# Layer 1 of a two-layer graph transformer on one NeuronCore: hand-laid memories, expert weights under tensors that end early, the residual assembled inside the second products, and routing by blocks

## The chip, the cores and the metric

The kernel runs on one NeuronCore of a Trainium2 chip, in one launch. The metric is device time in microseconds (us). Besides the run times there is one profiled execution of the kernel, whose trace gives the start and length of every instruction. Engines are named as the profile names them: PE is the matrix engine (PEld its weight loads), DVE the vector engine, ACT the scalar engine, POOL the general engine, SP the engine that here only starts DMA transfers; "SPq" or "POOLq" is such an engine's instruction queue.

## The reference, cut to what matters

Two layers work on x, 1250 rows of 512 numbers. Only the end of layer 1 is touched:

```python
xn = layernorm(x)
# graph part: agg is a 1250 x 1250 edge-count product
h  = (1 + eps) * xn + agg(xn)
h  = relu(batch_norm(h @ W1 + b1))      # 512 -> 1024, statistics over the 1250 rows
h  = relu(batch_norm(h @ W2 + b2))      # 1024 -> 512
gnn = xn + h
# slice attention, 8 heads of 64, 32 slices
xm = xn @ W_in + b_in
q, k, v = softmax(xm @ Wq), softmax_over_rows(xm @ Wk), xm @ Wv
mix = (q @ (k.T @ v)) @ W_out + b_out
x  = x + gnn + mix
# experts: each of 32 takes the 39 rows that the router scores highest for it
xf = layernorm(x)
S  = softmax(xf @ W_router + b_router)          # 1250 x 32
G, idx = top_k(S.T, 39)
up = xf[idx] @ W_up[group] + b_up               # 8 groups of 4 experts share W_up, 512 x 1365
y  = silu(up) @ W_down[expert] + b_down         # 32 matrices, 1365 x 512
x  = x.at[idx].add(G * y)
```

The expert weights are 8 W_up matrices of 2730 KB and 32 W_down matrices of 2816 KB (with their bias row). [...]

## The kernel before

A scheduler orders the instructions of each engine, mostly by the order of the program and by when operands are ready; inside a `manual_schedule` block the named engines keep the program's order. Each engine then runs its own queue in order and waits on semaphores. A tile pool is a piece of on-chip memory; a pool that is put where a released pool lay waits until the released pool's last reader is done. Pools on the "right" side grow from the top of the memory, and the tiles of one pool lie in it upwards in the order in which they are made.

The 1250 rows are ten tiles of 125 rows (`NT`, `TP`). `BLOCKS` groups them in 4, 4 and 2, so a block is 500, 500 or 250 columns of a transposed tensor. Four blocks of 128 features (`ND`) make 512; the 1024 hidden features are eight. A matrix product in float32 shows up as two PE records per matmul.

Layer 1 in order of time:

- **Preparation (L1099 to L1119).** SP loads the 1250 x 1250 count matrix `AT`, which has a pool of its own at the top of the memory. For each tile DVE computes the layer norm `xn3`; ACT rounds it to `xh`; POOL computes the remainder `xl = xn3 - xh` (L1118); PE transposes `xn3` to `xT`. Five `xn3` buffers rotate.
- **Aggregation (L1129)**: for each block and each 128 features, ten matmuls with `xh` and then ten with `xl` go into one PSUM bank; DVE adds `(1+eps) * xT`.
- **x_mid (L1149)**, then the **first products**: eight feature blocks `zT[m]` of the hidden layer, with the attention's pieces (`keys`, `queries_values`, `keys_values`) put between them on PE.
- **Second products (L1289 to L1303)**: four feature blocks of `gT`. For each, ACT adds the bias, DVE takes batch statistics (`batch_norm`), ACT applies the relu, and DVE adds `b_out` and `xT` (L1301).
- **finish(b) (L1319)**: for each tile, PE brings the four feature blocks of `gT` back to rows by matmuls with the identity (L1327) and adds the attention product `qsT @ kvW` in the same PSUM bank (L1329); DVE adds `xr` (L1330). Row statistics and the norm `xf` follow. POOL writes the row tile to `out` and `xf` to the DRAM tensor `xd`.
- **route(b) (L1340)**: PE transposes `xf`, multiplies with the router's weights (L170, 32 columns wide), and each tile goes through a softmax by itself; the 32 x 1250 scores end in `pT`. The finish of block n+1 stands ahead of the route of block n, and the scheduler may interleave them.
- **Top-k (L1382)**: five rounds on DVE, then the index tables, then the gather of the first token rows from `xd` (L1415).
- **Experts (L1426)**: per group 44 up matmuls (88 records) and 88 down matmuls of 39 rows (176 records), the weighted rows being added to `out` by an indirect DMA (L1458).

Eight slots of 22 KB per partition hold expert weights; `load(slots)` issues as many loads as the slots passed to it allow, in the order up, four downs, up, ... The first two slots (`expa`) are in the memory of the attention's temporaries, four (`expb`) where the 512 x 512 weights and `xr` lay, two (`expc`) where row tiles of the finish lay. A slot is loaded again when the matmuls that read it are done.

## Time and profile before

| | us |
|---|---|
| median of 3 runs | 1592.73 |
| lowest, highest | 1590.1, 1593.69 |
| the profiled execution, its own time | 1594.62 |
| its span (first to last instruction) | 1592.8 |

Landmarks in the profiled execution, from its timeline:

| what | from | to |
|---|---|---|
| aggregation on PE | 956.8 | 1004 |
| first products and attention pieces | 1047 | 1137.1 |
| second products | 1137.1 | 1206.4 |
| finish and route, until the top-k can start | 1206.4 | 1266.8 |
| top-k, index tables, first tokens | 1266.8 | 1299.5 |
| experts, first to last matmul | 1299.5 | 1576.7 |

Rows by stretch give for each engine the busy time and the number of instructions in brackets, then the granted PE clock (1.00 is full speed), the busy share of the DMA engines and what they moved in GB/s. Timeline rows give start, length, engine, line, operation, output<-inputs and count; what stands in square brackets is the idle time before it and what ended it. Group rows give busy time and mean length of one in ns, then the idle time ahead.

### The profile page before, as it was taken

How to read it: one execution, taken by the hardware profiler on the slowest of the kernel's cores; microseconds unless marked ns; L12 is line 12 of the kernel's file. 1: busy time of each engine (PE TensorE's matmuls, PEld its weight loads, DVE VectorE, ACT ScalarE, POOL GpSimd, SP SyncE). 2: the span in 40 equal slices, each digit the busy share in tenths (PEclk: the TensorE clock that was granted, in tenths of full speed). 3: DMA queues.
4: the chain of work that ended last, by engine and by line, in shares of the span. 5: the costliest groups of instructions: out<-in, count | busy, mean ns of one | idle time of the engine just before them, and what ended most of it. 6: DMA issues, size and time to landing. Idle time of an engine off the chain costs nothing. (4 is left out here: it accounts for less than half of the span.)

```text
span 1592.8 us, 15977 instructions
## 1 busy us (share of the span) xinstructions
PE 1450.2 (91%) x6218; PEld 783.2 (49%) x6218; DVE 670.5 (42%) x1476; ACT 400.9 (25%) x821; POOL 396.3 (25%) x308
## 2 busy tenths in 40 slices
PE   6999999999996999999999879999999649998895
PEld 3645744556664543222224338556655545564452
DVE  6313072457883453767667361245325430110000
ACT  1201110222332112444445310056321211111110
POOL 6100332000001200877787420000003102222111
PEclk9999999999997999999999999999999669999998
DMA  7100000001112300000000220000302589999994
GB/s 204 33 29 15 23 27 0 7 25 27 44 32 60 106 27 27 1 1 1 1 0 1 111 80 1 1 27 27 143 0 85 188 305 354 373 383 381 378 389 164
DMA packets 83009, 162.60 MB, mean 102 GB/s; under 512 B 17857, under 2 KB 19009, under 8 KB 82919
## 3 DMA queue, kind: packets, MB, share of 16 engines
q1 hardware_dynamic: 75031, 146.75, 25.9%
q0 software_dynamic: 6592, 14.44, 3.4%
q8 instruction: 54, 0.88, 0.2%
q10 hardware_dynamic: 1296, 0.23, 0.1%
q14 instruction: 36, 0.29, 0.1%
HBM read 147.48 MB, written 13.93 MB: 101 GB/s over the span
## 5 line engine op out<-in xcount | busy, mean ns | idle before, releaser
L937 POOL TENSOR_TENSOR acc<-acc,pT 125x1000 f32<-125x1000 f32 (+1 forms) x96 | 187.3, 1951 | 31.4 <-ACT pT L927 26.6
L1449 PE MATMUL ps_dn<-expw,act 128*39 128x512 f32 x704 | 161.9, 609 | 14.8 <-DMA expw<-in_W_down 14.8
L927 ACT ACTIVATE pT<-sc,sh 125x500 f32<-125x500 f32 (+1 forms) x240 | 132.7, 604 | 128.1 <-PE sc L919 118.4
L764 DVE TENSOR_REDUCE nms<-ps_nat 125x1 f32<-125x512 f32 (+1 forms) x240 | 128.5, 584 | 77.7 <-PE ps_nat L762 76.6
L919 PE MATMUL sc<-qT,kT 64*125 64x500 f32 (+1 forms) x480 | 117.9, 559 | 0.4 <-ACT sh L792 0.4
L945 PE MATMUL ps_o<-pT,va 125*64 125x500 f32 (+1 forms) x480 | 111.9, 545 | 0.0
L1449 PEld LDWEIGHTS ps_dn<-expw,act 128*39 128x39 f32 x704 | 44.0, 119 | 126.3 <-issue 107.0
L1435 PEld LDWEIGHTS ps_up<-tT,expw 128*128 128x128 f32 (+1 forms) x704 | 95.5, 191 | 6.6 <-issue 5.8
L1435 PE MATMUL ps_up<-tT,expw 128*128 128x156 f32 (+1 forms) x704 | 97.7, 302 | 0.5 <-ACT tT L1422 0.5
L1456 DVE TENSOR_SCALAR wgt<-ps_dn,pgat 39x512 f32<-39x512 f32 x32 | 24.0, 749 | 171.1 <-PE ps_dn L1449 170.6
L1458 POOL DMA_INDIRECT out_x<-wgt,sidx x32 | 45.3, 1417 | 182.1 <-DMA out_x<-wgt,sidx 88.1
L1438 ACT ACTIVATE act<-ps_up,vec 128x156 f32<-128x156 f32 (+1 forms) x88 | 34.3, 390 | 219.5 <-PE ps_up L1435 219.5
L513 DVE TENSOR_SCALAR os<-iota,smod,sval 125x626 bf16<-125x626 int16 x160 | 70.5, 441 | 3.8 <-PE ps_a L528 2.4
L163 PE MATMUL ps_f<-hT,l1w 128*128 128x500 f32 (+1 forms) x192 | 68.7, 513 | 0.0
L163 PE MATMUL ps_f<-zT,l1w 128*128 128x500 f32 (+1 forms) x192 | 67.6, 513 | 0.0
L528 PE MATMUL ps_a<-os,od 125*128 125x314 bf16 x392 | 66.1, 298 | 0.0
L919 PEld LDWEIGHTS sc<-qT,kT 64*125 64x125 f32 x480 | 36.9, 183 | 55.3 <-ACT pT L927 43.9
L762 PE MATMUL ps_nat<-kTr,qTr 64*125 64x512 bf16 (+1 forms) x240 | 49.1, 347 | 12.2 <-DVE nms L764 9.7
L828 POOL DMA_INDIRECT a_wk<-in_wk,rows x4 | 4.1, 1018 | 216.9 <-issue 216.9
L945 PEld LDWEIGHTS ps_o<-pT,va 125*64 125x64 f32 x480 | 24.3, 136 | 64.2 <-issue 63.9
L937 POOL TENSOR_TENSOR acc<-pT 125x1000 f32<-125x1000 f32 (+1 forms) x12 | 23.4, 1952 | 124.6 <-ACT pT L927 124.5
L163 PEld LDWEIGHTS ps_f<-zT,l1w 128*128 128x128 f32 x192 | 36.2, 189 | 31.1 <-issue 29.8
(365 smaller groups left out, 2239.3 us busy)
## 6 DMA issues: line engine op xcount, KB each, us to landing
expw<-in_W_down SPq DMA_DIRECT2D x28, 2816.0 KB
expw<-in_W_up SPq DMA_DIRECT2D x8, 2730.0 KB
expw<-in_W_down SPq DMA_DIRECT2D x4, 1536.0 KB
AT<-atd SPq DMA_DIRECT2D x9, 625.0 KB
atd<-ATd SPq DMA_DIRECT2D x10, 546.9 KB
expw<-in_W_down SPq DMA_DIRECT2D x4, 1280.0 KB
l1w<-in_l_W SPq DMA_DIRECT2D x4, 1024.0 KB
out_x<-x2r POOLq DMA_DIRECT2D x10, 224.0 KB, 2.7
```

Of the source, the lines that this page charges most:

```text
L163: nc.tensor.matmul(ps[:, :width], w(k)[:, m * P:(m + 1) * P], xT(k), start=k == 0, stop=k == nk - 1)
L513: nc.vector.tensor_scalar(oss[c % len(oss)][:, :HN + 1], iota[:TP, :HN + 1], smod[:, c:c + 1], sval[:, c:c + 1], ALU.is_equal, ALU.mult)
L528: nc.tensor.matmul(pss[d][:, n, :HALF], ods[c][:, a:a + P], oss[c % len(oss)][:, n * HALF:(n + 1) * HALF], start=c == CHUNKS[d][0], stop=c ...
L762: nc.tensor.matmul(pss[e][:TP, :z - y], qTr[r, c, i * TP:(i + 1) * TP], kTr[r, c, y:z], start=True, stop=True)
L764: nc.vector.tensor_reduce(nms[n][:, j, e, a:a + 1], pss[e][:TP, :z - y], AX.X, ALU.max)
L919: nc.tensor.matmul(scs[n, k][e][:, :w], kT[r, c, k * TP:(k + 1) * TP], qT[r, c, span(b)], start=True, stop=True)
L927: nc.scalar.activation(pT[:, e, :w], sc[:, :w], AF.Exp, bias=shs[n])
L937: nc.gpsimd.tensor_tensor(a, pTs[n, 0][:, :, :w] if k == 1 else a, pTs[n, k][:, :, :w], ALU.add)
L945: nc.tensor.matmul(os_[n][e * DH:(e + 1) * DH, :w], vn[:, k, h * DH:(h + 1) * DH], pTs[n, k][:, e, :w], start=k == 0, stop=k == NT - 1,)
L1435: nc.tensor.matmul(ps[:fw, :4 * CAP], wu[:, k, f * P:f * P + fw], tT[:, k, :], start=k == 0, stop=k == ND - 1)
L1449: nc.tensor.matmul(ps[j * 64:j * 64 + CAP, :], act[:, f, (2 * a + j) * CAP:(2 * a + j + 1) * CAP], expw["down", pair][j][:, f, :], start=f ...
L1458: nc.gpsimd.indirect_dma_start(out=out[:, :], out_offset=bass.IndirectOffsetOnAxis(ap=sidx[:CAP, e:e + 1], axis=0), in_=wgt[r, :], in_offs ...
```

## The change

The tensors of layer 1 and the expert slots no longer have pools of their own. Three memories are laid out by hand: `bm` (which holds `xr` and the four 512 x 512 weight places), `lb` and `la`. `at(m, a, ...)` is a view into one of them. There are again eight slots, now lying under tensors that end at different times:

- slot 1 under `xT`, 2 under `xmT` and a part of `kn`, 3 under the attention's temporaries, 4 under `qsT` and `kvW`, 5 under most of `zT`, 6 under three weight places, 7 under `gT`, 8 under `xr`;
- `load(1)` stands behind x_mid, `load(3)` behind the first products, `load(4)` in the second products, `load(6)` behind them, `load(8)` behind the routing. Down matrices are loaded one by one rather than in pairs.

`AT` now shares the pool `xn3p` with `xh`, `xl` and the five `xn3` buffers. `xT` is no longer needed at the end: POOL adds `xn3` to `xr` in the preparation. In the second products PE also does the attention product of each tile (`attended`) and the transposes of each finished feature block (`rows`), and DVE adds both to `xr` and takes the statistics in pieces of 128 features. After the last feature block come the row statistics of all ten tiles together and then, block by block, `normed` and `route`; the softmax handles a block at once. This part now stands inside the `manual_schedule` of PE. The last hidden block `zT[7]` lies where the second half of `l1_W1` lay, so its three bias steps are held back until that block's products are done.

```diff
-    resp = tc.alloc_tile_pool(name="resp", bufs=1)
+    base = ctx.enter_context(tc.tile_pool(name="base", bufs=1))
...
+    bm = base.tile([P, NT * D + 4 * ND * D], F32, name="bm")
+    xr = bm[:TP, :NT * D].rearrange("p (i d) -> p i d", d=D)
...
+    SLOT = NF * D
+    lb = ctx.enter_context(tc.tile_pool(name="l1memb", bufs=1)).tile([P, 2 * SLOT], F32, name="lb")
+    REST = 4 * SLOT
+    BREST = SLOT
+    LOADS = [w for g in range(NG) for w in (("up", g), *(("down", 4 * g + j) for j in range(4)))]
...
-        atp = tc.alloc_tile_pool(name="atp2", bufs=1, side="right")
-        AT = atp.tile([P, NT, N], F32, name="AT1")
+        xp = tc.alloc_tile_pool(name="xn3p", bufs=1, side="right")
+        AT = xp.tile([P, NT, N], F32, name="AT1")
...
+        xh = xp.tile([TP, NT, D], F32R, name="xh3")
+        xl = xp.tile([TP, NT, D], F32R, name="xl3")
...
+                nc.gpsimd.tensor_tensor(xl[:, i, :], xn[i], xh[:, i, :].bitcast(F32), ALU.subtract)
+                nc.gpsimd.tensor_tensor(xr[:, i, :], xr[:, i, :], xn[i], ALU.add)
...
+        la = ctx.enter_context(tc.tile_pool(name="l1mema", bufs=1)).tile([P, REST + 3736], F32, name="la")
+        SLOTS = [at(m, a, SLOT) for m, a in (
+            (lb, 0), (la, 0), (la, SLOT), (la, 2 * SLOT), (la, 3 * SLOT), (bm, NT * D + 4 * ND * D - SLOT), (lb, SLOT), (bm, 0)
+        )]
...
+        load(1)
...
+                    while held and (m < 2 * ND - 1 or b == BLOCKS[-1]):
+                        b_, ps = held.pop(0)
+                        nc.scalar.activation(zT[m][:, span(b_)], ps, AF.Identity, bias=v_("b1", m))
...
+            load(3)
+            def attended(i):
+                s = slice(i * TP, (i + 1) * TP)
+                mm_N(
+                    psum, [(qsT[:, j, s], kvW[:, j, :]) for j in range(2)],
+                    lambda ps: nc.vector.tensor_add(xr[:, i, :], xr[:, i, :], ps),
+                )
+            def rows(m, b):
+                ps = psum.tile([TP, 4, P], F32, name="ps_x", tag="mm")
+                v = xr[:, b[0]:b[0] + b[1], m * P:(m + 1) * P]
+                for i in tiles_of(b):
+                    nc.tensor.transpose(ps[:, i - b[0], :], gT[:, m, i * TP:(i + 1) * TP], ident)
+                nc.vector.tensor_add(v, v, ps[:, :b[1], :])
+                for i in tiles_of(b):
+                    nc.vector.bn_stats(st[:, i, m, :], xr[:, i, m * P:(m + 1) * P])
+            todo = [(attended, i) for i in range(NT)]
...
+                    if m and b == BLOCKS[0]:
+                        todo += [(rows, m - 1, b_) for b_ in BLOCKS]
+                    for _ in range(2 if m == 0 else 3):
+                        if todo:
+                            f, *x = todo.pop(0)
+                            f(*x)
+                    if m == 1 and b == BLOCKS[-1]:
+                        load(4)
...
-                    nc.vector.scalar_tensor_tensor(
-                        gT[:, m, span(b)], gT[:, m, span(b)], v_("b_out", m), xT[:, m, span(b)], op0=ALU.add, op1=ALU.add
-                    )
+                    nc.vector.tensor_scalar(gT[:, m, span(b)], gT[:, m, span(b)], v_("b_out", m), None, ALU.add)
+            load(6)
...
+            for b in BLOCKS:
+                rows(ND - 1, b)
+            for i in range(NT):
+                nc.vector.bn_aggr(mv[:, i, :], st[:, i, :, :])
+            nc.scalar.activation(rs[:, :, 0], mv[:, :, 1], AF.Sqrt, bias=eps5[:TP])
...
+            def normed(b):
+                for i in tiles_of(b):
+                    xf = xfs[i] = at(bm, BREST + i % 4 * D, D, p=TP)
+                    if i % 2:
+                        nc.scalar.activation(xf, xr[:, i, :], AF.Identity, bias=rs[:, i, 1:2], scale=rs[:, i, 0:1])
+                    else:
+                        norm(xf, xr[:, i, :], mv, rs[:, :, 0], i)
+                for i in tiles_of(b):
+                    put_rows(xd, i, xfs[i])
+                    put_rows(out, i, xr[:, i, :])
...
+                for i in range(n):
+                    for k in range(ND):
+                        nc.tensor.matmul(
+                            ps[:, i, :], xfT[:, k, i * TP:(i + 1) * TP], wr[:, k, :], start=k == 0, stop=k == ND - 1
+                        )
...
+                nc.vector.tensor_tensor(pr, ps[:, :n, :], bias.to_broadcast([TP, n, NE]), ALU.add)
+                nc.vector.tensor_reduce(su[:, :, 0], pr, AX.X, ALU.max)
+                nc.vector.tensor_tensor(pr, pr, su.to_broadcast([TP, n, NE]), ALU.subtract)
+                nc.scalar.activation(pr, pr, AF.Exp)
+                nc.vector.tensor_reduce(su[:, :, 0], pr, AX.X, ALU.add)
                 nc.vector.reciprocal(su, su)
-                nc.vector.tensor_scalar(pr, pr, su, None, ALU.mult)
+                nc.vector.tensor_tensor(pr, pr, su.to_broadcast([TP, n, NE]), ALU.mult)
...
+            for b in BLOCKS:
+                normed(b)
+                route(b)
+    load(len(SLOTS))
...
-        load(sum(ROOM) + 5 * g + 1)
+        load(len(SLOTS) + 5 * g + 1)
...
-            load(sum(ROOM) + 5 * g + 2 * a + 3)
+            load(len(SLOTS) + 5 * g + 2 * a + 3)
```

In the expert stage `tok`, `act`, `tT` and `wgt` become views into `la` and `bm` with the same number of buffers as before.

## The prediction

> **What bounds the kernel now.** I read the page's slices first, then the engines by stretch, then the groups, the timeline around each stage boundary, and the granted clock in steps of 2 us.
>
> ```profile
> PEclk9999999999997999999999999999999669999998
> DMA  7100000001112300000000220000302589999994
> GB/s 204 33 29 15 23 27 0 7 25 27 44 32 60 106 27 27 1 1 1 1 0 1 111 80 1 1 27 27 143 0 85 188 305 354 373 383 381 378 389 164
> ```
>
> One slice is 39.8 us. DMA is nearly idle until slice 31 (it begins at 1195 us) and full from slice 34 (1314) on: the expert weights are the only heavy transfer, and they come late. The clock drops in slices 32 and 33, which hold the end of the routing and the top-k.
>
> ```profile
> 1137.00:1208.00 71.00, 71.00 (x219) 38.50 (x219) 18.85 (x51) 15.78 (x26) 0.37 (x3) 1.00 0.22 80
> 1208.00:1267.00 59.00, 48.97 (x237) 36.70 (x235) 31.46 (x94) 16.23 (x42) 21.82 (x41) 0.79 0.43 141
> 1267.00:1299.00 32.00, 1.93 (x10) 1.39 (x10) 22.10 (x33) 0.42 (x1) 2.94 (x3) 0.50 1.02 379
> 1299.00:1346.00 47.00, 46.50 (x282) 32.35 (x284) 3.74 (x6) 10.89 (x26) 7.39 (x7) 0.95 0.83 290
> 1472.00:1535.00 63.00, 54.89 (x305) 30.00 (x306) 5.46 (x8) 8.31 (x22) 10.71 (x9) 0.96 1.05 382
> ```
>
> The second products (first row) are pure PE: 71.00 of 71. Finish and route (second) keep PE busy for 49 of 59 us, so PE sets most of that too. Top-k and gather are DVE and latency. The experts start on PE and end on DMA (1.05 busy, 382 GB/s).
>
> ```profile
> 1313.71 0.37 SPq L1075 DMA_DIRECT2D expw<-in_W_down  x1
> 1323.82 0.37 SPq L1075 DMA_DIRECT2D expw<-in_W_down  x1
> ```
>
> These are the loads number nine and ten. The first up products run from 1299.5 to 1313.7, the first down pair to 1323.7: each of these loads goes out the moment its slot is read out. DMA was idle between about 1307 and 1314 because all eight slots were full. From then on 32 loads stream until the last down product can start at 1572.2: 258.5 us, 8.1 us each.
>
> **The change, part by part.** I compare the start T of the first up product (1299.5 now) and then the expert stage.
>
> *Expert stage: 0.* Eight slots before, eight after, and the ninth load still waits for the first up products: T+14.2, as now. What is loaded earlier is the first eight, and they are complete at T+8 already today, earlier than PE reads them. So the stream still ends 272.7 us after T and the stage keeps its 277.2 us. The single loads instead of pairs change nothing here: the rows above show that a pair already goes out one matrix at a time. If this were wrong, the price is 277.2 - 8 x 31.42 (one group on PE: 11.86 + 0.54 + 19.01) = 26 us, 2.3 of it the slow first up products.
>
> *Preparation: +8.* Each tile gets a second POOL instruction.
>
> ```profile
> 945.07 13.23 POOL L1118 TENSOR_TENSOR xl<-xn,xh 125x512 fp32r<-125x512 f32 x10 [4.05 <-ACT xh L1117]
> 956.75 3.73 PE L1129 MATMUL ps_ag<-AT,xh 125*128 125x500 f32 x10
> 960.31 2.45 PE L1129 MATMUL ps_ag<-AT,xl 125*128 125x500 f32 x10
> ```
>
> POOL has no gap in its ten subtractions, and the last ends at 958.3, just ahead of its use. A two-input add of 125x512 takes 1.265 us on POOL (the residual add of layer 0, L427). In program order the adds stand between the subtractions; I take them to alternate, so the tenth subtraction ends near 945.1 + 19 x 1.31 = 970. It is needed by the tenth `xl` matmul, which now ends at 962.6. The wait is about 8 us, and part of it runs into a slow PE clock afterwards. Five `xn3` buffers slow the norms as well (tile 9 at about 959), but this lies within the same wait. If all adds fell behind the subtractions, another step would be late next:
>
> ```profile
> 903.42 5.54 SPq L1099 DMA_DIRECT2D AT<-atd  x9
> ```
>
> `AT` now shares a pool with tiles that reach down over the attention's operands, which the output projection reads until 940.4. Its load takes 18.5 us (903.4 to 921.9), so it would land at 959 to 962 with the weight load beside it, against a first use at 956.75: at least +3. With the POOL wait it is hidden. The weight loads behind `AT` in SP's queue are needed only from 1004 on. Range +3 to +12. `load(1)` waits in SP's queue only for the reads of `xT`, about when the next weight's load behind it comes free anyway.
>
> *First products: 0.* The held bias steps add about 1.2 us of ACT behind the last matmul. The relu of `zT[7]` runs now at 1139.2 to 1140.6, and PE needs it at 1137.1 + 7 x 0.85 = 1143. This slack is the cover; without it the cost is 1.2.
>
> *Second products: +20.4.* PE has no gap there, so everything put in costs its full time.
>
> ```profile
> L1329 PE MATMUL ps_x<-kvW,qsT 128*125 128x512 f32 x40 | 19.9, 617 | 0.0
> L1327 PE MATMUL ps_x<-ident,hT 128*125 128x128 f32 x80 | 11.6, 291 | 0.4 <-DVE hT L1301 0.4
> L156 PE MATMUL ps_t<-ident,xf 125*128 125x125 f32 x40 | 6.3, 300 | 0.0
> L170 PE MATMUL ps_n<-wr,xT 128*125 128x32 f32 x80 | 15.7, 359 | 0.0
> ```
>
> (Matmuls overlap, so I use their spacing, not the mean.) The attention products take 1.72 us a tile in the timeline: 17.2. The 30 transposes of three feature blocks replace identity matmuls of two records each; a transpose is one record, spaced 0.107: 3.2. DVE's additions (0.69 each) lie beside. The products end at 1206.4 + 20.4.
>
> *Behind the products: from 60.4 to 51, -9.4.* The time now is 1206.4 to 1266.8. Afterwards, from the end E of the products:
> - The batch norm of the last feature block is ready at E+4.1 to E+5.2, as now.
> - DVE then adds three blocks (1.7), takes ten statistics of 128 (about 0.29, on the line through 0.68 at 500 and 0.42 at 250: 2.9), and aggregates ten tiles (0.18 at 6 values, 0.23 at 18, so 0.25 at 24: 2.4): E+12.2. Root, reciprocal and product with their hand-offs: E+13.1. Two norms on DVE (0.48) beside two on ACT (0.62): E+14.4. PE has next to nothing to do for these 14 us.
> - A block of four: 16 transposes, the last copy 0.6, 16 logit matmuls (32 records), the softmax 2.5 (six DVE steps of about 0.25, one ACT step of 0.35, hand-offs), four transposes. PE keeps the program's order, so block 1's transposes wait for block 0's softmax; the finish that filled these gaps is gone.
>
> What a record costs depends on the clock:
>
> ```profile
> 1236.00:1238.00 2.00, 2.00 (x11) 2.00 (x12) 0.19 (x1) 0.20 (x2) 0.23 (x1) 0.50 0.52 167
> 1240.00:1242.00 2.00, 2.00 (x6) 0.94 (x6) 0.24 (x1) 0.00 (x0) 0.00 (x0) 0.50 0.01 4
> 1244.00:1246.00 2.00, 2.00 (x10) 1.11 (x9) 1.30 (x3) 0.00 (x0) 1.06 (x2) 1.00 0.10 27
> ```
>
> After a gap at 1230 to 1233.5 PE was fully busy, yet it stayed at 0.50 for 8 us of narrow logit matmuls, and came back only when the 512-wide `ps_x` matmuls ran. [...] By the row (0.21 and 0.21) a block of four is 3.4 + 0.6 + 6.7 + 2.5 + 0.9 = 14.1, the last 8.3: 14.4 + 28.2 + 8.3 + 0.4 = 51. I take the row, because the 512-wide matmuls have left this stretch. Range 41 to 56.
>
> POOL's queue: 40 DMA issues of 0.54 (L1317) as now, 2.1 us a tile from E+14 on; with four `xf` buffers tile 7 can be written when tile 3's copy has landed, near E+25, ahead of its transposes at E+28. The gather at about E+73 finds the queue empty. SP's last early load waits for the `out` writes and ends before the top-k does.
>
> *Gather: -3.* Top-k and tables keep their 24 us. The second token gather is issued at 1291.6 and read at 1298.2, 6.6 us under full DMA; the indirect loads of layer 0, with DMA quiet, land in 3.6 (L828). Range -4 to -2.
>
> **Sum**, against the profiled execution: +8 + 20.4 - 9.4 - 3 + 0 = +16.0. Its own time, 1594.62, is 1.9 above the median, so I add to the median: 1592.7 + 16 = 1608.7. About 0.2%, 3.2 us, is what a measurement of this kernel can tell from no change.
>
> **Rivals.**
> [...]
> - *The expert stage loses its waits.* Place: the second down pairs of groups 4 to 6, where PE waits for DMA (4 waits, 14.8 us recorded, 23.6 with what runs stretched). Price: -23.6, total -7.6: 1585. It decides once the stream runs 16 us, two loads, further ahead than now. For it: the first eight slots are full long before T. Against it: the ninth load at 1313.71 already waits for nothing but its slot.
> - *It does not do what it says.* If waits cover a whole memory rather than the region, early loads do not start and each later one waits for all readers: 1650 or more. Against it: PE began the second products at 1137.09 while ACT was to write another part of the one tile `zT` until 1140.6.
>
> **How the numbers follow.** Main case 0.60; short tail 0.25, of it 0.05 within 0.2% and 0.02 below; expert stage 0.10; whole-memory waits 0.05. Faster 0.12, same 0.05, slower 0.83. The main case by its bounds reaches from +4 to +26. The range 1595 to 1619 takes in the short tail above 1595 and leaves out the expert case, the whole-memory case and the lowest part of the short tail, together 0.2.
>
> **What would show it.** Right: a first `xl` group on PE that ends near 970; `AT` issued at 940; second products of 90 us; a tail of 51 us at clock 0.50; the ninth load 14 us behind the first up product. Wrong: a ninth load closer to T, a tail near 41, or no gap ahead of the aggregation.

## The result and the profile after

The changed kernel takes 1598.29 us (median of 5 runs, 1597.21 to 1603.3) against 1591.73 us for the kernel before on the same chip: a ratio of the means of 1.0048 [1.0029, 1.0066], 7.6 us slower (6.6 between the medians). A second measurement gave 1.0069 [1.0056, 1.0082], 11 us. The direction was as forecast; of the 16 us, about half came in the first measurement and two thirds in the second. The profiled execution of the changed kernel took 1603.3 us, the upper end of its runs, so it is compared by stages, as is each experiment.

The page's slices, to be laid over those of before (a slice is 40.0 us):

```profile
PEclk9999999999997999999999979999999569999998
DMA  7100000011112300000000050020412809999994
GB/s 203 33 33 25 9 27 0 7 30 28 38 37 63 97 27 27 1 1 1 1 0 2 2 187 1 1 97 27 144 51 87 337 29 346 374 378 381 378 388 164
```

Slices 27 to 32, counted from 1, now carry the early expert loads (up to 337 GB/s). Slice 33, in which DMA ran at 305 GB/s before, has only 29: all eight slots are full and the stream waits. From slice 34 on the two profiles are alike.

The same five stretches as before, moved to where the stages now lie (busy time and count for PE, PEld, DVE, ACT and POOL, then clock, DMA share, GB/s):

```profile
1144.00:1234.00 90.00, 89.90 (x272) 47.31 (x271) 33.34 (x98) 15.16 (x25) 0.00 (x0) 1.00 0.18 66
1234.00:1278.00 44.00, 28.14 (x140) 25.75 (x140) 19.92 (x67) 12.15 (x21) 21.75 (x41) 0.58 0.90 334
1278.00:1307.00 29.00, 2.12 (x11) 1.58 (x12) 22.05 (x33) 1.06 (x3) 3.25 (x4) 0.50 0.20 74
1307.00:1354.00 47.00, 47.00 (x284) 32.85 (x286) 3.89 (x6) 10.24 (x25) 7.08 (x7) 0.94 0.69 242
1480.00:1543.00 63.00, 54.81 (x309) 30.44 (x309) 5.46 (x8) 8.41 (x22) 10.71 (x9) 0.96 1.05 382
```

The second products fill 90 us with PE busy throughout, the tail has shrunk to 44 us with PE busy for 28, the gather reads at a DMA share of 0.20 instead of 1.02, and the expert stage is what it was: 54.81 busy in 63 us against 54.89. The ninth and tenth load:

```profile
1321.57 0.37 SPq L1094 DMA_DIRECT2D lb<-in_W_down  x1
1331.67 0.37 SPq L1094 DMA_DIRECT2D la<-in_W_down  x1
```

The first up product starts at 1306.8, so the ninth load goes out 14.8 us behind it (14.2 before). Stage by stage:

| stage | before | after | forecast | measured |
|---|---|---|---|---|
| preparation to first products (from the output projection's end) | 196.8 | 204.5 | +8 | +7.8 |
| second products | 69.4 | 89.9 | +20.4 | +20.5 |
| tail, to the start of the top-k | 60.3 | 43.9 | -9.4 | -16.4 |
| top-k and gather | 32.7 | 29.0 | -3 | -3.7 |
| experts, first up to last down matmul | 277.2 | 278.5 | 0 | +1.3 |

Ahead of layer 1 the changed kernel's execution is 0.9 ahead. The tail is the only step off by more than 1.3 us.

### The profile page after: what moved, and what is told of

Same layout as the page of the kernel before. It is cut to its first block, busy times and chain, and to the rows that moved or that the text cites. A ratio compares the mean times of both kernels' runs of the same rounds, so it can differ in the third digit from the quotient of the medians.

```text
span 1601.5 us, 15961 instructions
## 1 busy us (share of the span) xinstructions
PE 1451.5 (91%) x6178; PEld 784.8 (49%) x6178; DVE 677.1 (42%) x1496; ACT 396.2 (25%) x799; POOL 409.3 (26%) x318
## 5 line engine op out<-in xcount | busy, mean ns | idle before, releaser
L172 PE MATMUL ps_f<-x2T,bm 128*128 128x500 f32 (+1 forms) x288 | 104.0, 518 | 2.3 <-DVE x2T L421 1.7
L172 PE MATMUL ps_f<-lb,bm 128*128 128x500 f32 (+1 forms) x288 | 102.3, 513 | 1.6 <-issue 1.6
L1503 PE MATMUL ps_dn<-la 128*39 128x512 f32 x352 | 99.8, 606 | 3.7 <-DMA la<-in_W_down 3.7
L1512 POOL DMA_INDIRECT out_x<-bm,sidx x32 | 45.3, 1417 | 182.7 <-DMA out_x<-bm,sidx 87.1
L1492 ACT ACTIVATE la<-ps_up,vec 128x156 f32<-128x156 f32 (+1 forms) x88 | 34.3, 390 | 220.7 <-PE ps_up L1489 220.7
L1503 PE MATMUL ps_dn<-lb,la 128*39 128x512 f32 x176 | 79.2, 607 | 6.9 <-DMA lb<-in_W_down 6.9
L1503 PE MATMUL ps_dn<-bm,la 128*39 128x512 f32 x176 | 80.7, 616 | 5.1 <-DMA bm<-in_W_down 5.1
L172 PEld LDWEIGHTS ps_f<-x2T,bm 128*128 128x128 f32 x288 | 54.5, 191 | 49.0 <-issue 40.1
L172 PEld LDWEIGHTS ps_f<-lb,bm 128*128 128x128 f32 x288 | 54.0, 189 | 48.5 <-issue 44.4
L172 PE MATMUL ps_f<-la,bm 128*128 128x500 f32 (+1 forms) x168 | 60.9, 513 | 0.0
L771 PE MATMUL ps_nat<-kTr,qTr 64*125 64x512 bf16 (+1 forms) x240 | 49.0, 347 | 12.2 <-DVE nms L773 9.7
```

The costliest lines, as they stand in the source:

```text
L172: nc.tensor.matmul(ps[:, :width], w(k)[:, m * P:(m + 1) * P], xT(k), start=k == 0, stop=k == nk - 1)
L771: nc.tensor.matmul(pss[e][:TP, :z - y], qTr[r, c, i * TP:(i + 1) * TP], kTr[r, c, y:z], start=True, stop=True)
L1503: nc.tensor.matmul(ps[j * 64:j * 64 + CAP, :], act[:, f, (2 * a + j) * CAP:(2 * a + j + 1) * CAP], expw["down", 2 * pair + j][:, f, :], st ...
L1512: nc.gpsimd.indirect_dma_start(out=out[:, :], out_offset=bass.IndirectOffsetOnAxis(ap=sidx[:CAP, e:e + 1], axis=0), in_=wgt[r, :], in_offs ...
```

## The experiments

Stage times below are from one profiled execution each, ratios from four or more timed runs. The first run repeats the changed kernel; it shows how much the stages move by themselves.

> The changed kernel once more, as the yardstick for the others. Its one profiled execution so far lay at the upper end of its five runs (span 1601.5 against 1595.4 to 1601.5). If that is scatter, this one's profile shows the same stages: second products from about 204.5 us after the end of the output projection and 89.7 long, 44 from their end to the top-k, 29 from there to the first up product, about 293 from there to the end. If one stage scatters, that stage alone is shorter here. Time 1597 to 1600.

The stages came again within 1.4 us; the time, 1601.62 us, lay a little above the range.

| run | ratio to before | preparation | products | tail | experts |
|---|---|---|---|---|---|
| changed kernel again | 1.0069 [1.0056, 1.0082] | 204.2 | 89.9 | 42.5 | 279.7 |
| DVE adds | 1.0047 [1.0032, 1.0063] | 199.5 | 89.9 | 45.6 | 278.1 |
| DVE adds, own `AT` | 1.0047 [1.0029, 1.0065] | 199.3 | 89.9 | 45.7 | 278.6 |
| pipelined | 1.0052 [1.0039, 1.0065] | 202.5 | 89.9 | 45.2 | 279.4 |
| extra matmuls | 1.0054 [1.0039, 1.0070] | 204.2 | 89.9 | 42.4 | 278.2 |
| two held back | 1.0041 [1.0028, 1.0055] | 204.3 | 86.5 | 44.6 | 279.1 |
| ten held back | 1.0035 [1.0023, 1.0047] | 204.0 | 72.7 | 56.2 | 279.3 |
| two loads fewer | 1.0040 [1.0026, 1.0055] | 202.7 | 89.9 | 43.9 | 276.9 |
| adds late | 1.0020 [1.0010, 1.0029] | 200.4 | 89.9 | 42.9 | 276.8 |
| pipelined, extra matmuls | 1.0038 [1.0025, 1.0051] | 204.3 | 89.9 | 42.6 | 277.8 |
| no early `load` calls | 1.0052 [1.0037, 1.0066] | 202.6 | 89.9 | 45.2 | 280.0 |
| first combination | 1.0000 [0.9990, 1.0010] | 198.6 | 86.5 | 44.2 | 277.3 |
| adds late, own `AT` | 1.0015 [1.0001, 1.0028] | 196.5 | 89.9 | 45.7 | 277.4 |
| reordered | 1.0018 [1.0006, 1.0030] | 204.6 | 89.9 | 41.2 | 280.1 |
| second combination | 0.9923 [0.9905, 0.9940] | 196.5 | 83.0 | 38.2 | 278.0 |

### The preparation: GpSimd's second pass, and what it hid

In the changed kernel POOL adds and subtracts in turns, and PE waits for the last two remainders (timelines of POOL and of PE):

```profile
940.79 6.90 POOL L1143 TENSOR_TENSOR bm<-bm,xn 125x512 f32<-125x512 f32 x5 [0.45 <-DVE xn L158]
...
960.81 3.77 POOL L1143 TENSOR_TENSOR bm<-bm,xn 125x512 f32<-125x512 f32 x3
964.53 2.48 POOL L1141 TENSOR_TENSOR xl<-xn,xh 125x512 fp32r<-125x512 f32 x2
```

```profile
965.85 0.50 PE L1154 MATMUL ps_ag<-AT,xl 125*128 125x500 f32 x1 [1.43 <-POOL xl L1141]
967.07 0.50 PE L1154 MATMUL ps_ag<-AT,xl 125*128 125x500 f32 x1 [0.72 <-POOL xl L1141]
```

POOL works without a gap from 940.8 to 967.0, and the first `xl` group ends near 967.4, before at 962.6; counted from the output projection's end that is 5.7 us later. In PE's time, 2.2 of these are the two waits shown and 3.4 a later start of the aggregation: the first five norms on DVE take 5.22 instead of 2.36 us beside POOL's additions, and the next ones wait 0.6 us longer for a buffer (timelines of DVE, before and after):

```profile
940.98 2.36 DVE L149 TENSOR_SCALAR xn<-xr,mv,rs 125x512 f32<-125x512 f32 x5
```

```profile
940.10 5.22 DVE L158 TENSOR_SCALAR xn<-bm,mv,rs 125x512 f32<-125x512 f32 x5
```

With POOL's twenty instructions in a row, an earlier start would only have lengthened the waits. The next two runs move the additions to DVE, where they become one affine step `xr * (1 + rs) - mean * rs`, and the second also gives `AT` a pool of its own:

```diff
-                nc.gpsimd.tensor_tensor(xr[:, i, :], xr[:, i, :], xn[i], ALU.add)
...
+            for i in tiles_of(b):
+                nc.vector.tensor_scalar(xr[:, i, :], xr[:, i, :], rs[:, i:i + 1], mr[:, i:i + 1], ALU.mult, ALU.subtract)
```

```diff
+        atp = tc.alloc_tile_pool(name="atp2", bufs=1, side="right")
+        AT = atp.tile([P, NT, N], F32, name="AT1")
         xp = tc.alloc_tile_pool(name="xn3p", bufs=1, side="right")
-        AT = xp.tile([P, NT, N], F32, name="AT1")
```

> The residual add of the preparation leaves POOL: DVE computes xr * (1 + rs) - mean * rs behind the norms (ten times about 0.5 us, while PE runs the first aggregation group). Theory A, POOL's second pass makes the aggregation late: POOL's ten subtractions run without gaps again, and the wait shrinks from 7.7 us to what the late load of AT alone costs, 4 to 5 (AT lands near 961, and with AT there PE must do ten xh and ten xl matmuls), so 3 to 4 us faster. Theory B, AT alone sets it: no change, within 1 us. If the adds cost nothing and AT nothing: 7.7 faster.

> As the run before it, and AT in a pool of its own at the top of the memory again, so that its load can start when the attention ends, at about 903, and not at 940. Theory A: the preparation is back at the time of before: 7 to 8 us faster than the changed kernel, of which AT alone is 4. Theory B (AT sets all of it): also 7 to 8 faster, but the run before this one did nothing. A third: AT's late load was hidden altogether, and this run equals the one before it.

Only 5.0 of the 7.8 us came back, and `AT`'s earlier load (issued at 900.5 instead of 939.6) gave nothing, the third of the cases above. The rest had a new cause. The scheduler put the additions ahead of the last tiles' norms (timeline of DVE in the second of these runs):

```profile
946.82 4.30 DVE L1152 TENSOR_SCALAR bm<-bm,rs,mr 125x512 f32<-125x512 f32 x3
951.05 1.22 DVE L1150 TENSOR_SCALAR rs<-rs 125x4 f32<-125x4 f32 x1
...
953.29 0.99 DVE L158 TENSOR_SCALAR xn<-bm,mv,rs 125x512 f32<-125x512 f32 x2
```

So the additions went further back, behind the aggregation in the program, with `1 + rs` and `mean * rs` kept:

```diff
         load(1)
+        for i in range(NT):
+            nc.vector.tensor_scalar(xr[:, i, :], xr[:, i, :], sm[:, i, 0:1], sm[:, i, 1:2], ALU.mult, ALU.subtract)
```

> The changed kernel with GpSimd's second pass taken out of the preparation and the additions made by VectorE (ten affine instructions of about 0.6 us) behind the aggregation, beside the projection into the mixer, where VectorE has idle time. Theory (the whole loss of the preparation is the second pass, first as GpSimd's work and then, in the run with VectorE's additions, as additions that went ahead of the last norms): the aggregation starts 16.4 us behind the output projection as before the change, the preparation falls from 204.5 to 196 to 198 us, the run by 6 to 8 us. Rival (the aggregation's memories or the late load of the adjacency carry part of it): it stays at 199 us or above.

The aggregation now starts 16.5 us behind the output projection, as before the change, yet the preparation is still 3.6 us over that of before, as the rival said. The timeline of PE has the reason:

```profile
958.21 0.47 PE L1156 MATMUL ps_ag<-AT,xh 125*128 125x500 f32 x1 [1.90 <-DMA AT<-atd]
958.51 3.98 PE L1156 MATMUL ps_ag<-AT,xl 125*128 125x500 f32 x10
```

PE waits for the last part of `AT`, and its next group takes 3.98 instead of 2.45 us; the like group of the changed kernel took 3.99 at clock 0.55. The load that cost nothing two runs earlier is bare. With `AT` in its own pool as well:

> The run with VectorE's additions behind the aggregation, and the adjacency in memory of its own that is free some 35 us earlier. There the preparation still stood 3.6 us over the kernel before, with 1.9 us of TensorE's idle time put down to the adjacency's load and a first group at half clock. Theory (the late load was hidden only by GpSimd's second pass and is bare without it): no such wait is left, the preparation falls from 200.4 to 196 to 197.5 us, the tail and the second products stay, the run 3 to 4 us shorter. Rival (the late load costs nothing here either, and the 3.6 us lie in the first products): it stays within 1 us of 200.4.

```profile
954.13 3.48 PE L1157 MATMUL ps_ag<-AT,xh 125*128 125x500 f32 x10
957.45 2.43 PE L1157 MATMUL ps_ag<-AT,xl 125*128 125x500 f32 x10
```

There is no wait left and the stage takes 196.5 us, 0.3 below the kernel before. The theory is right for the stage: without POOL's second pass the preparation is 4.1 us shorter than in the changed kernel, and `AT`'s own pool then takes off another 3.9. In the trace of the changed kernel no matmul waits for `AT`; its lateness lies within POOL's. (`AT`'s own pool beside POOL's additions was not run.) In the timed runs this last step does not show (1.0020 and 1.0015, with intervals that overlap); in its profiled execution the tail was 2.7 us longer, with the same instructions.

### The second products

Attended products of the last tiles are held back and put behind the products; `LATE` is the last two tiles or all ten. In these two kernels the held products read operands that an early weight load has by then overwritten; number, shape and length of the instructions are the same.

```diff
-            todo = [(attended, i) for i in range(NT)]
+            todo = [(attended, i) for i in range(NT - 2)]
...
+            for i in LATE:
+                attended(i)
+                for m in range(ND - 1):
+                    nc.vector.bn_stats(st[:, i, m, :], xr[:, i, m * P:(m + 1) * P])
             for b in BLOCKS:
                 rows(ND - 1, b)
```

> The changed kernel with the attended products of the last two tiles taken out of the second products and put behind them, in TensorE's idle 4 us ahead of the last columns' transposes, with these tiles' statistics. Theory (a product in the second products costs its 1.72 us in full, one in that gap nothing): second products 89.9 to 86.5 us, tail unchanged within 1 us, the run 3.4 us shorter. Rival (the six bn_stats and two additions that go with them delay the aggregation on VectorE): the tail grows by 2 to 4 us and the run is the same within 1 us.

> The changed kernel with all ten attended products and the additions of them behind the second products, so that this part of the change is undone and the routing by blocks alone is left. Theory (the 17.2 us are TensorE's own time and only change their place, apart from the 4 us gap that they fill): second products 89.9 to 72.7 us, tail 43.9 to 56 to 58 us, the run 3 to 5 us shorter than the changed kernel. Rival (the tail's gain of 16.4 us came from the routing by blocks alone, and the attended products were no part of the tail of before): the tail stays under 50 us and the run falls by over 10 us.

Both theories hold for the stages. Two products less take 3.4 us off the stage, ten take 17.2 off. With all ten held back the products stand at 72.7, 3.3 over the kernel before: the price of the transposes, for which 3.2 was forecast. The tail then grows by 12.3, not by 17.2, since the first of them fill PE's wait behind the products. The DVE work that goes with two tiles does delay the first block a little (its transposes wait 5.91 instead of 4.62 us).

### The tail: order, buffers and clock

In the changed kernel's tail, from the end of the products at 1233.9 (first the timeline of DVE, then that of PE):

```profile
1241.53 1.25 DVE L1335 BATCH_NORM_STATS2 st<-bm 125x6 f32<-125x128 f32 x6
1242.70 1.34 DVE L1374 BATCH_NORM_AGGREGATE mv<-st 125x2 f32<-125x24 f32 x10
...
1244.75 1.00 DVE L158 TENSOR_SCALAR bm<-bm,mv,rs 125x512 f32<-125x512 f32 x2
```

```profile
1245.44 3.98 PE L165 MATMUL ps_t<-ident,bm 125*128 125x125 f32 x16 [4.62 <-DVE bm L158]
1249.21 6.77 PE L1404 MATMUL ps_lg<-wr,la 128*125 128x32 f32 x32
1258.31 0.99 PE L1421 MATMUL ps_pt<-ident,rpr 125*32 125x125 f32 x4 [2.33 <-DVE rpr L1418]
1259.09 2.98 PE L165 MATMUL ps_t<-ident,bm 125*128 125x125 f32 x16
1261.91 4.75 PE L1404 MATMUL ps_lg<-wr,la 128*125 128x32 f32 x32
```

The first block's 32 logit records take 6.77 us, the second block's 4.75: the clock was back from 1261.4 to 1264.8. The first try was to put the next block's transposes ahead of a block's softmax, with a second set of buffers for `xf`; the second, to fill PE's two waits with matmuls whose result nobody reads:

```diff
             for b in BLOCKS:
                 normed(b)
-                route(b)
+                turned(b)
+                if n:
+                    scores(BLOCKS[n - 1])
+                logits(b)
+            scores(BLOCKS[-1])
```

> The routing in another order on PE: block n+1's transposes stand ahead of block n's softmax transposes, and the second block's normed rows have buffers of their own. Theory A, PE stands idle behind each block's softmax because its order is fixed (2.3 us twice) and behind a buffer that waits for its copy to DRAM: the part from the end of the second products to the top-k falls from 44 to about 38, 5 to 6 us faster. Rival: with the clock at half, DVE's and ACT's copies between the transposes set the pace, and the softmax moves behind them: less than 2 us.

```diff
+            for _ in range(4):
+                ps = psum.tile([P, 512], F32, name="ps_warm", tag="mm")
+                nc.tensor.matmul(ps, ident, gT.rearrange("p c n -> p (c n)")[:, :512], start=True, stop=True)
             for b in BLOCKS:
                 rows(ND - 1, b)
```

and five more of the same behind the rows.

> The changed kernel with nine matmuls of 128 x 512 fp32 added that compute nothing that is used: four ahead of the last columns' transposes and five behind them, so that TensorE works through the 4 us behind the second products and the 4.6 us ahead of the first block's transposes. Theory (the clock fell to .50 in those idle stretches, and the tail is TensorE's at that clock): the first block's transposes take 0.11 instead of 0.21 us and its 32 logit matmuls 0.15 instead of 0.21 us each, the tail falls from 43.9 to 36 to 40 us, the run by 4 to 8 us. Rival (the clock is not kept up by such work, or the small work itself lets it fall): the clock reads .50 through the blocks as before, the tail is unchanged or up to 4 us longer.

Neither moved the time: 45.2 and 42.4 us, within what the unchanged tail shows. In the pipelined run PE still waits 1.6 and 1.7 us for the first two softmaxes (2.3 each before), and all blocks ran at clock 0.50. In the run with the extra matmuls the first block's logits took 3.85 us, and what PE gained there it then lost waiting for the softmax. DVE's row shows why:

```profile
1252.33 0.59 DVE L158 TENSOR_SCALAR bm<-bm,mv,rs 125x512 f32<-125x512 f32 x1 [5.32 <-DMA xd<-bm]
1252.84 0.27 DVE L1418 TENSOR_TENSOR rpr<-ps_lg,misc 125x128 f32<-125x128 f32 x1
```

Tile 4's norm stands ahead of block 0's softmax in DVE's queue and waits until the write of the old rows to `xd` has left one of the four buffers. A faster PE ends in this wait. Both together:

> The changed kernel with both of two earlier changes: the next block's transposes ahead of a block's softmax with a second set of buffers for the normed rows, and the nine extra matmuls around the last columns' transposes. Theory (each alone moved the bound: with the clock up VectorE waited for the buffers that the writes to memory held; with the buffers the clock stayed at .50; together both are gone): the tail falls from 42.4 to 43.9 to 35 to 39 us. Rival (the clock falls to .50 within some 10 us of narrow matmuls whatever goes before): 41 us or more.

The rival's number came (42.6): the clock was 1.00 until 1248 and then 0.50 again. Here it helps to compare the executions whose tails have the same instructions. The 32 logit records of blocks 0 and 1, and the 16 of block 2, took:

| execution | block 0 | block 1 | block 2 | tail |
|---|---|---|---|---|
| changed kernel | 6.77 | 4.75 | 3.41 | 43.9 |
| changed kernel again | 6.77 | 4.44 | 2.22 | 42.5 |
| DVE adds | 3.93 | 6.77 | 3.41 | 45.6 |
| DVE adds, own `AT` | 3.98 | 6.77 | 3.41 | 45.7 |
| two loads fewer | 6.77 | 4.76 | 3.41 | 43.9 |
| adds late | 4.06 | 3.99 | 3.41 | 42.9 |
| no early `load` calls | 6.77 | 6.77 | 2.14 | 45.2 |
| adds late, own `AT` | 3.92 | 6.77 | 3.41 | 45.7 |

The same code gets the full clock in one block or another, and a fast first block does not even shorten the tail, because DVE's wait takes it back (PE waits 4.8 us for `rpr` in the adds-late run, 2.33 in the changed kernel). So in this order of instructions the tail lies between 42.5 and 45.7 us whichever block gets the full clock.

When the clock returns can be read from the traces. Their record of the granted clock changes only at the ends of steps of 3.41 us: the 24 changes in the changed kernel's trace, all between 0.50 and 1.00, lie whole numbers of such steps apart, and so do the 24 in the trace of the kernel before. Four such steps of the changed kernel, the last two following each other:

```profile
1244.29:1247.70 3.41, 2.24 (x9) 1.73 (x10) 1.98 (x5) 1.61 (x3) 1.08 (x3) 0.50 1.01 416
1251.12:1254.53 3.41, 3.41 (x18) 3.41 (x18) 0.55 (x1) 0.21 (x1) 2.65 (x5) 0.50 1.05 414
1257.94:1261.35 3.41, 3.04 (x15) 2.90 (x16) 1.57 (x3) 0.76 (x2) 2.51 (x6) 0.50 1.05 413
1261.35:1264.77 3.42, 3.42 (x31) 3.24 (x30) 1.14 (x2) 1.44 (x3) 1.77 (x4) 1.00 1.03 390
```

In the second, PE was busy throughout with logits alone, and the clock stayed at 0.50; in the third it was busy for 3.04 us with transposes, and the next step ran at 1.00. Between 1220 and 1280 us the sixteen traces of the changed kernel and its variants hold 197 steps at half clock. The 163 with under 2.3 us of transposes were all followed by another at half clock, among them 23 with at least 3 us of logits. The 8 with over 2.9 us of transposes were all followed by full clock. Of the 26 between, 9 were. So in these traces a PE busy with 32-wide logits did not bring the clock back (23 steps of 23), and a block's transposes did where over 2.9 us of them fell into one step (8 of 8): the first block's were split into 2.24 and 1.51 us in the changed kernel, and 3.22 us of them lay in one step in the adds-late run. The extra matmuls did hold the clock up: it fell 3.6 us behind the products' end in the changed kernel, and 17.9 and 17.8 us behind it in the two runs with nine of them. Which measure of PE's work counts, and what sets where the steps lie, stays open.

What is left is order. The next run moves the logits too ahead of the previous block's softmax, with the second buffers and without extra matmuls:

```diff
                 turned(b)
+                logits(b)
                 if n:
                     scores(BLOCKS[n - 1])
-                logits(b)
             scores(BLOCKS[-1])
```

> The changed kernel with a second set of buffers for the normed rows, and in TensorE's order the next block's transposes and also its logits ahead of a block's softmax transposes, so that nothing of the routing but the last softmax stands between TensorE's instructions; no extra matmuls. Theory (with all gaps closed the tail is TensorE's sum at clock .50: 16.3 us from the start of the first block's transposes to the first block's end of two blocks' worth, then 6 and the last softmax): the tail is 39 to 42 us. Rival (the clock is what decides, and without a gap it stays at .50 where gaps let it come back): 43 us or more.

```profile
1244.92 3.98 PE L165 MATMUL ps_t<-ident,bm 125*128 125x125 f32 x16 [4.62 <-DVE bm L158]
1248.69 6.77 PE L1410 MATMUL ps_lg<-wr,la 128*125 128x32 f32 x32
1255.27 3.57 PE L165 MATMUL ps_t<-ident,lb 125*128 125x125 f32 x16
1258.64 7.01 PE L1410 MATMUL ps_lg<-wr,la 128*125 128x32 f32 x32
1265.46 1.02 PE L1431 MATMUL ps_pt<-ident,rpr 125*32 125x125 f32 x4
```

PE has no gap from 1244.9 to the last softmax, and the tail is 41.2 us although every block ran at half clock. The pipelined run, also at half clock throughout, took 45.2, so the order is worth 4 us at an equal clock. The theory holds for the stage. The ratio fell to 1.0018 [1.0006, 1.0030], the largest effect of a change to the tail alone. That is 5 to 8 us under the changed kernel's two ratios, while the profiled tail is 1.3 to 2.7 shorter; the profiled execution was the slowest of the twelve, and what the others gained beyond it is not shown.

### The expert stage

> The changed kernel without the last two of the 40 weight loads: experts 30 and 31 use the down matrices of experts 28 and 29, their own are left out. Theory (the expert stage is bound by the stream of weights, whose loads behind the routing take 10.1 us each): the time from the first up product to the last down matmul falls from 278.5 by 14 to 20 us, TensorE's own work being under it. Rival (TensorE bounds the stage and the loads run ahead of it): it falls by under 4 us.

The stage fell by 1.6 us, which favours the rival and is no more than this stage scatters by (276.8 to 280.1 us in the runs with all loads). The run was also badly placed. PE's waits for loads lie in the middle of the stage and are still there (they add up to 15.7 us in the changed kernel, 14.8 before); the two loads left out are the last ones of the stream and touch only its end. It says that the last two loads bound little, and nothing on the middle.

The other run takes out the calls `load(1)`, `load(3)`, `load(4)` and `load(6)`, so that all eight loads stand behind the second products in the program:

> The changed kernel with the early weight loads put behind the second products, all eight at once, so that the layout by hand gives no early load. Theory (eight loads take 60 to 80 us at the full rate, 73 us lie between the products' end and the first up product, and only the last ones are late): the expert stage grows by 0 to 8 us and the tail by 0 to 3 through slower row writes. Rival (the early loads are what the layout buys, and without them the stream is late for good): the expert stage grows by over 20 us.

The loads went out where they had gone out before (timelines of SP, the changed kernel first):

```profile
1045.95 0.40 SPq L1090 DMA_DIRECT2D lb<-in_W_up  x1
...
1131.92 100.69 SPq L1094 DMA_DIRECT2D la<-in_W_down  x4
```

```profile
1045.36 0.45 SPq L1090 DMA_DIRECT2D lb<-in_W_up  x1
...
1130.83 100.69 SPq L1094 DMA_DIRECT2D la<-in_W_down  x4
```

SP runs ahead and is held only by the readers of what lies in a slot; where the call stands does not matter here. Neither theory was put to a test, and the kernel is the changed one in effect (1.0052).

### Two combinations

> The changed kernel with the additions behind the aggregation (as in the first of these runs), the attended products of the last two tiles behind the second products, with the fourth early load moved behind them since their operands lie where it lands, the next block's transposes ahead of a block's softmax with a second set of buffers, and five extra matmuls behind the last columns' transposes. Theory (the three losses are separate and add up): 7.7 less in the preparation, 3.4 less in the second products, 3 to 6 less in the tail, the run 14 to 17 us under the changed kernel and 6 to 9 us under the one before it. Rival (what is saved ahead of the expert stage is lost in it, since its loads start late): the run equals the kernel before within 3 us.

This one joins the late additions, two held tiles, the pipelined order and five extra matmuls. It equals the kernel before (1.0000 [0.9990, 1.0010]), as the rival said, but not for the rival's reason: its expert stage is 277.3. What was missing is 2 us of `AT`'s wait and the tail, 44.2, which the pipelined order does not shorten.

The second joins what the runs had shown: late additions, `AT` in its own pool, the reordered tail with second buffers, and four tiles held back. Two of these fill PE's wait behind the products; two go behind the last columns' transposes, and DVE adds them and takes their statistics behind the first two blocks' norms:

```diff
+            def last_two():
+                for i, ps in zip(LATE[2:], behind):
+                    nc.vector.tensor_add(xr[:, i, :], xr[:, i, :], ps)
+                    for m in range(ND):
+                        nc.vector.bn_stats(st[:, i, m, :], xr[:, i, m * P:(m + 1) * P])
+                means(NT - 2, NT)
...
                 normed(b)
+                if n == 1:
+                    last_two()
                 turned(b)
```

> The changed kernel with four edits: the additions on VectorE behind the aggregation; the adjacency in memory of its own; the attended products of the last four tiles behind the second products (two in TensorE's wait there, two behind the last columns' transposes with their additions and statistics put behind the first two blocks' norms), the fourth early load and those behind it moved behind them; and the order of transposes and logits of the run before this one. Theory (the losses are separate): preparation 196 to 197.5, second products 83, tail 40 to 44, the run 1583 to 1587, which is 5 to 9 us under the kernel before. Rival (what VectorE now does behind the products delays the first block's rows by more than TensorE saves): tail over 46 us, the run within 3 us of the kernel before.

```profile
1216.36 3.60 PE L179 MATMUL ps_n<-la 128*125 128x512 f32 x8
1220.90 0.67 PE L1338 MATMUL ps_x<-ident,lb 128*125 128x128 f32 x4 [0.94 <-DVE lb L1365]
1221.88 0.89 PE L1338 MATMUL ps_x<-ident,lb 128*125 128x128 f32 x6 [0.31 <-DVE lb L1365]
1222.61 3.60 PE L179 MATMUL ps_n<-la 128*125 128x512 f32 x8
1228.12 0.88 PE L165 MATMUL ps_t<-ident,bm 125*128 125x125 f32 x3 [1.91 <-DVE bm L158]
```

1580.86 us (median of 6, 1577.48 to 1581.53), a ratio of 0.9923 [0.9905, 0.9940]: 12 us under the kernel before, and the only version that beats it. Held products have taken the place of most of the 3.81 and 4.62 us waits, the products are down to 83.0 and the tail to 38.2, better than forecast. The clock has a part in this: it was 0.75 of full speed over this tail against 0.54 in the reordered run, and the first two blocks' logits took 4.04 and 4.34 us against 6.77 and 7.01. With the held products on PE the clock first fell 12.2 us behind the products' end. How much of the gain is order and how much clock was not separated.

## Why the prediction was right or wrong

- *Preparation, +8: right* (+7.8). It was to be a wait for the last `xl`, with `AT`'s delay hidden behind it. Both are shown: no matmul in the trace of the changed kernel waits for `AT`, and once POOL's adds were gone, the own pool gave 3.9 us, near the "at least +3" of the text. The first `xl` group ended at 967.4, not 970 (5.7 us later than before, not 8), since POOL's first instruction was an addition, which does not wait for `xh` and began at 940.8 instead of 945.1. The group behind it, at clock 0.55, took 1.5 us longer (3.99 instead of 2.45). The text names this slow clock but gives it no size, so that the sum fits so closely is in part luck.
- *First products, 0.* No run took the held bias steps out by themselves; with the preparation mended the whole stretch took 196.5 against 196.8, so they cost nothing that can be seen.
- *Second products, +20.4: right* (+20.5), and in its parts: 17.2 and 3.3 by the run with ten held back.
- *Tail, -9.4: wrong* (-16.4). This term failed, by 7 us, in four places. (1) The start of the first block was put at E+14.4 from the products' end E; it was E+11.5. A `bn_aggr` over 24 values was extrapolated to 0.25 us from the lengths of single ones; ten in a row took 1.34 us, 0.13 each, which is 1.1 less. A `bn_stats` of 128 was taken as 0.29 and took 0.21 (1.25 for six), 0.8 less for ten. And PE did not wait for all four norms (1.3): it began 0.7 behind the start of the first. (2) The first block, from its transposes to the next block's, was put at 14.1 and took 13.65. (3) The second took 10.7 instead of 14.1: in this execution its clock came back; in the run without early `load` calls, where it did not, it took 13.2. (4) The last block and the copy took 8.05 instead of 8.7. Some 5 us are thus steps sized too long, the largest part of them DVE's statistics, with durations read off as if each instruction stood alone, and about 2.5 are the clock.
- *The clock.* The 51 was added up at the row's 0.21 a record, thus at 0.50 throughout (its 0.4 is the copy to `pT`). The low end of the range, 41, was the author's estimate for a tail mostly at full clock, from the spacings of the kernel before at 1.00: 16 transposes in 1.87 us, 8 logit records in 1.23 (1227.70 and 1229.41 in its timeline of PE). No run shows such a tail in the changed kernel's order of instructions: its own had a clock of 0.58, and the eight profiled ones took 42.5 to 45.7. Nor did 51 come. PE was busy almost without a break from 1246 to 1256 while the clock stayed at 0.50, and at 1262 it had the full clock on the same narrow work, which the row excludes (granted clock in the column ahead of the DMA share):

```profile
1250.00:1252.00 2.00, 2.00 (x11) 2.00 (x11) 0.00 (x0) 0.03 (x1) 1.09 (x3) 0.50 1.01 403
1254.00:1256.00 2.00, 1.98 (x10) 1.84 (x9) 0.00 (x0) 1.66 (x2) 1.61 (x3) 0.50 1.05 413
1262.00:1264.00 2.00, 2.00 (x18) 1.82 (x17) 0.82 (x2) 0.57 (x1) 0.71 (x2) 1.00 1.00 384
```

  The row was also misread: of its 8 us only 5 were logits (1233.6 to 1238.5). Then came products of 128 and of 512 columns, and the clock was back at 1242.7, at the end of the first step of 3.41 us without logits. Transposes 125 wide, which the tail kept, were followed by the same (3.04 us of them in the step from 1257.94, shown with the tail's experiments).

- *Gather, -3:* right (-3.7). *Experts, 0:* right within 1.3, which is less than this stage scatters by; the ninth load came 14.8 us behind the first up product and waited for its slot only.
- *The rivals.* The short tail (0.25), a tail of 41 with +4 for the preparation, was put at about 1597, close to the measured time, but neither term came: the adds did cost their 8, and the tail came to 44 rather than 41. The closeness is luck. The expert stage did not lose its waits, and the memories are tracked by region, not whole: the early loads did start early, the first at 1045.95 and the next from 1131.92 on. A slip in the sum: the lowest bounds of the terms (+3, +20.4, -19.4, -4) add up to 0, not to +4.

## What to carry to other kernels

Moving work from a tail into a stage where one engine has no gap cost its full length there (17.2 us here); it pays only if the tail loses as much, so look for the tail's own waits and move into these only as much as fills them (here four products of ten). A cost hidden behind another came out when the first was removed (3.9 us of `AT`'s here), so try the two mends together before calling either useless. And where the granted clock switches within a stage, read it in several executions before building on one, step by step against what PE did in each step.

## What was not expected of the hardware

- TensorE's clock stayed at 0.50 through about 24 us of almost gapless transposes and 32-wide matmuls (1246 to 1270 in the reordered run), while the same instructions ran at 1.00 in some blocks of other executions. Busy time is not what counted: in the sixteen traces, steps with at least 3 us of 32-wide logits were followed by half clock, 23 of 23. In the reordered run no step of 3.41 us in these 24 us held more than 2.2 us of transposes, and each was followed by half clock, as were all 163 such steps with under 2.3 us.
- The affine step on DVE took 0.46 us a tile (4.18 for nine) while POOL was idle, and 1.43 (4.30 for three) while POOL ran its subtractions. The norms show the same: five took 2.36 us without POOL's work, three 4.29 beside it, and five 5.22 beside the additions of the changed kernel. What holds DVE up there was not tested.
- Ten `bn_aggr` of 24 values in a row took 1.34 us.
